# Placing the operands of the attention products 64 bytes apart modulo 128 in an fp32r kernel with split operands

## The chip, the cores and the metric

One core of a Trainium2 chip. The metric is the device time of one execution in microseconds (us), the median of several runs. TensorE (PE) does the matmuls, PEld is its weight load, VectorE is DVE, ScalarE is ACT, GpSimd is POOL. All runs quoted here were in the fast state, with a granted clock of 0.997 to 0.999. Ratios are the mean time of one kernel's fast runs over that of the other's of the same rounds, so not quite the ratio of the medians that stand beside them. The rounds of the experiments ran on three chips, so kernels of different rounds are compared through their ratios.

## The reference

```python
q = einsum('bwhc,cd->bwhd', x, Wq) + bq          # x: (4, 64, 64, 256), q and k: 128 channels
k = einsum('bwhc,cd->bwhd', x, Wk) + bk
v = einsum('bwhc,cd->bwhd', x, Wv) + bv
pq, pk, pv = (t.reshape(B, -1, 4096) for t in (q, k, v))
attention = softmax(einsum('bcn,bcm->bnm', pq, pk), axis=-1)
out = einsum('bcm,bnm->bcn', pv, attention).reshape(B, W, H, C)
return gamma * out + x
```

Four images, 4096 queries and 4096 keys each.

## The kernel before

Each operand is split in three forms, called h, l and d, of the program's type fp32r (the trace lists it as f32), and each product is made of three. For every image 16 groups of 256 queries are worked off, each in 8 **units** of 512 keys. One unit is 36 matmuls on TensorE: 12 of q·k (three forms, four key blocks), then 8 each of vh·h, vl·l and vd·d, in that order. In the matmul call the first argument after the output is the weights and the second is what is streamed, so k and h, l, d are weights and q and vh, vl, vd are streamed.

```python
VC = C + 4                                   # C = 256
...
pool("pad", 1).tile([P, 16], F32, name="pad")
ppool, work, kpool = pool("ppool", 2), pool("work", 2), pool("kpool", 3)
...
vh = qkv.tile([P, NM, VC], F32R, tag="vh", name="vh")
vl = qkv.tile([P, NM, VC], F32R, tag="vl", name="vl")
vd = qkv.tile([P, NM, C], F32R, tag="vd", name="vd")
...
def energy(b, u, k):                         # q.k, half a unit
    ...
    for i in range(2):
        for to, f, first, last in ((sa, 0, True, False), (sa, 1, False, True), (sb, 2, True, True)):
            nc.tensor.matmul(
                to[:, i], kt[:, 2 * k + i, f, :], q[:, :, f, :], start=first, stop=last
            )
...
def attend(b, u):                            # v.p, one unit
    ...
    for left, right in ((h, vh), (l, vl), (d, vd)):
        for j in range(NJ):                  # two blocks of 128 queries
            out_ = bb[:, j, :] if left is d else acc[j]      # acc is 258 wide, bb 256
            for i in range(4):
                m = 2 * t + i // 2 + NI * (i % 2)
                nc.tensor.matmul(
                    out_,
                    left[:, i, j * P : (j + 1) * P],
                    right[:, m, : out_.shape[1]],
                    ...
                )
```

Rows of vh and vl end in two columns of ones, which give the softmax sums. That is why their products have 258 columns and those of vd and q·k 256.

## Time and profile before

| | before |
|---|---|
| median | 2495.41 us (2495.35 to 2495.9) |
| PE busy, PEld busy | 99%, 98% |
| DVE, ACT busy | 85%, 73% |
| matmul records | 19,982, of them 18,432 in q·k and v·p |

The lines that carry this are in the prediction below. Two readings come before it. A busy time of PE is overlapped latency, so the pace has to be read from where matmuls start. And the timeline merges equal neighbours: a row says when the first of eight started, so the next row's start minus this one's, over eight, is the pace. These are the starts of vh in four successive units of the kernel before (timeline of TensorE, start us, us, engine, line, operation, tile and shape, count):

```profile
218.72 1.11 PE L368 MATMUL a<-vh,h 128*128 128x258 f32 x8
...
222.98 1.13 PE L368 MATMUL a<-vh,h 128*128 128x258 f32 x8
...
227.23 1.11 PE L368 MATMUL a<-vh,h 128*128 128x258 f32 x8
...
231.46 0.76 PE L368 MATMUL a<-vh,h 128*128 128x258 f32 x5
```

The units last 4.26, 4.25 and 4.23 us: they are not all alike. This small fact turned out to be the key.

### The profile page before, as it was taken

The page shows a single profiled execution, that of the slowest core. Times are in us where ns is not written, and L with a number is a line of the kernel's source. Part 1 is how long each engine was busy: PE and PEld are TensorE (multiplying, and loading weights), DVE is VectorE, ACT ScalarE, POOL GpSimd, SP SyncE. Part 2 cuts the span into 40 slices and gives each one's busy share as a digit, 9 for nine tenths or more (in the row PEclk, how much of TensorE's full clock was granted, in tenths as well). Part 3 has the DMA queues.
Part 4 walks back from the last instruction along what each step waited for, and adds up shares of the span by engine and source line. Part 5 has one row for each costly group of instructions (what it writes and reads, how often), then busy time and mean ns, then how long its engine had stood idle before and what let it go on. Part 6 is the DMA issues. An engine that isn't in the chain of part 4 may idle for free.

```text
span 2492.0 us, 50085 instructions
## 1 busy us (share of the span) xinstructions
PE 2478.3 (99%) x19982; PEld 2436.0 (98%) x19982; DVE 2108.0 (85%) x2440; ACT 1808.3 (73%) x3138; POOL 425.0 (17%) x780
## 2 busy tenths in 40 slices
PE   9999999999999999999999999999999999999998
PEld 8999999999899999999989999999998999999998
DVE  5888888888698888888869888888886988888887
ACT  5777777776677777777667777777766777777775
POOL 4211111111411111111041111111114111111110
PEclk9999999999999999999999999999999999999999
DMA  7766666664766666666477666666648666666663
GB/s 238 219 193 211 200 205 198 195 208 150 239 216 195 205 201 205 203 192 207 137 245 222 200 192 208 203 207 196 191 145 253 216 201 198 200 204 207 199 192 110
DMA packets 137408, 498.92 MB, mean 200 GB/s; under 512 B 15536, under 2 KB 57264, under 8 KB 137168
## 3 DMA queue, kind: packets, MB, share of 16 engines
q0 software_dynamic: 92320, 453.17, 57.8%
q1 hardware_dynamic: 44304, 42.22, 5.7%
q8 instruction: 160, 2.62, 0.4%
q14 instruction: 80, 0.66, 0.1%
q10 hardware_dynamic: 544, 0.26, 0.0%
HBM read 445.25 MB, written 50.33 MB: 199 GB/s over the span
## 4 chain that ended last, share of the span: by engine, by line
PE 97%; ACT 2%; DVE 1%; issue 0%; DMA 0%; SPq 0%; ACTq 0%; DVEq 0%
PE a L368 38%; PE sa L318 19%; PE bb L368 19%; PE sb L318 10%; PE qk L136 4%; PE v L157 4%; PE ot L414 1%; PE xt L123 1%; ACT h L337 1%; DVE x L332 1%; ACT x L322 0%; ACT y L322 0%; DMA x<-in_x_dram 0%; DVE vd L285 0%; ACT vh L282 0%
## 5 line engine op out<-in xcount | busy, mean ns | idle before, releaser
L322 ACT ACTIVATE x<-sa 128x512 f32<-128x512 f32 x1024 | 608.2, 594 | 399.7 <-PE sa L318 386.4
L318 PE MATMUL sa<-q,k 128*128 128x256 f32 x4096 | 755.0, 282 | 0.7 <-ACT x L322 0.7
L332 DVE TENSOR_TENSOR x<-x,y 128x1024 f32<-128x1024 f32 x512 | 625.3, 1221 | 152.9 <-ACT y L322 152.9
L318 PEld LDWEIGHTS sa<-q,k 128*128 128x128 f32 x4096 | 627.8, 189 | 2.1 <-ACT x L322 1.5
L343 DVE TENSOR_TENSOR l<-x,h 128x1024 fp32r<-128x1024 f32 x512 | 623.5, 1218 | 0.0
L346 DVE SCALAR_TENSOR_TENSOR d<-h,x 128x1024 fp32r<-128x1024 f32 x512 | 623.4, 1218 | 0.0
L322 ACT ACTIVATE y<-sb 128x512 f32<-128x512 f32 x1024 | 612.8, 598 | 0.0
L318 PE MATMUL sb<-q,k 128*128 128x256 f32 x2048 | 580.7, 284 | 0.0
L368 PE MATMUL a<-vh,h 128*128 128x258 f32 x4096 | 576.6, 283 | 0.0
L368 PE MATMUL a<-vl,l 128*128 128x258 f32 x4096 | 574.2, 283 | 0.0
L337 ACT ACTIVATE h<-x 128x1024 fp32r<-128x1024 f32 x512 | 543.6, 1062 | 41.1 <-DVE x L332 37.9
L368 PE MATMUL bb<-vd,d 128*128 128x256 f32 x4096 | 559.9, 279 | 0.0
L302 POOL DMA_DIRECT2D k<-kf x512 | 280.0, 547 | 1485.3 <-PE sb L318 1466.7
L368 PEld LDWEIGHTS a<-vl,l 128*128 128x128 f32 x4096 | 526.9, 190 | 0.0
L368 PEld LDWEIGHTS a<-vh,h 128*128 128x128 f32 x4096 | 524.0, 189 | 0.0
L368 PEld LDWEIGHTS bb<-vd,d 128*128 128x128 f32 x4096 | 515.1, 189 | 0.0
L318 PEld LDWEIGHTS sb<-q,k 128*128 128x128 f32 x2048 | 385.4, 188 | 9.6 <-ACT y L322 3.3
L136 PE MATMUL qk<-wqk_sb,xts 128*128 128x256 f32 x512 | 121.3, 380 | 0.0
L398 DVE SCALAR_TENSOR_TENSOR o<-a,o 128x256 f32<-128x256 f32 x126 | 47.5, 419 | 87.2 <-ACT o L378 87.2
L157 PE MATMUL v<-xts,wv_sb 128*128 128x256 f32 x512 | 120.3, 379 | 0.0
L157 PEld LDWEIGHTS v<-xts,wv_sb 128*128 128x128 f32 x512 | 97.3, 190 | 13.2
L406 ACT ACTIVATE o<-o,r 128x256 f32<-128x256 f32 x126 | 57.4, 503 | 72.4 <-DVE r L389 72.4
(54 smaller groups left out, 927.7 us busy)
## 6 DMA issues: line engine op xcount, KB each, us to landing
k<-kf POOLq DMA_DIRECT2D x512, 768.0 KB, 4.7
x<-in_x_dram SPq DMA_DIRECT2D x128, 256.0 KB, 3.7
kf<-f POOLq DMA_DIRECT2D x64, 384.0 KB, 3.9
out_dram<-x POOLq DMA_DIRECT2D x63, 256.0 KB, 2.5
qd<-qks POOLq DMA_DIRECT2D x128, 64.0 KB, 3.0
qr<-qd SPq DMA_DIRECT2D x64, 128.0 KB, 3.0
wv_sb<-in_L_conv_Wv_dram POOLq DMA_DIRECT2D x1, 256.0 KB, 6.1
out_dram<-x SPq DMA_DIRECT2D x1, 256.0 KB, 3.7
```

Of the source, the lines that this page charges most:

```text
L136: nc.tensor.matmul(qk[:, s, :], self.xt[i][:, k, s, :], wqk_sb[:, k, :], start=(k == 0), stop=(k == KC - 1),)
L157: nc.tensor.matmul(vp[:, eh, :], wv_sb[:, k, eh * P : (eh + 1) * P], self.xt[i][:, k].rearrange("p s a -> p (s a)"), start=(k == 0), stop= ...
L302: nc.gpsimd.dma_start(t.rearrange("p (i s) f d -> p i s (f d)", s=2), kf[b, u % NU])
L318: nc.tensor.matmul(to[:, i], kt[:, 2 * k + i, f, :], q[:, :, f, :], start=first, stop=last)
L322: nc.scalar.activation(to[:, 2 * k : 2 * k + 2, :], sp.rearrange("p i j d -> p i (j d)"), AF.Exp, scale=scale,)
L332: nc.vector.tensor_tensor(x, x, y, ALU.mult)
L337: nc.scalar.activation(h, units[b, u], AF.Identity, scale=UPPER)
L343: nc.vector.tensor_tensor(l, x, h.bitcast(F32), ALU.subtract)
L346: nc.vector.scalar_tensor_tensor(d, h.bitcast(F32), 1.0 + E, x, ALU.mult, ALU.subtract)
L368: nc.tensor.matmul(out_, left[:, i, j * P : (j + 1) * P], right[:, m, : out_.shape[1]], start=(t == i == 0 and (left is h or left is d and ...
L398: nc.vector.scalar_tensor_tensor(o[:, j, :], a[:, :C], 1.0 + E, o[:, j, :], ALU.mult, ALU.add)
L406: nc.scalar.activation(o[:, j, :], o[:, j, :], AF.Identity, scale=r[:, j : j + 1])
```

## The change

The intent: make the distance between the two operands of every product 64 bytes modulo 128. Rows of 1152 bytes for vh and vl take 7 KB per partition more, so k's forms move into buffers of l and d, which are free while k is made, and the raw q has one buffer instead of two.

```diff
-    VC = C + 4
+    VC = C + 32
...
-        ppool, work, kpool = pool("ppool", 2), pool("work", 2), pool("kpool", 3)
+        ppool = pool("ppool", 2)
+        pool("pad2", 1).tile([P, 16], F32, name="pad2")
+        work, kpool = pool("work", 2), pool("kpool", 3)
...
-            f = kpool.tile([P, 2, 3, P], F32R, tag="f", name=f"f_{b}_{i}", bufs=2)
+            f = ppool.tile([P, 4, NB], F32R, tag="ld"[i % 2], name=f"f_{b}_{i}")
+            f = f.rearrange("p i n -> p (i n)")[:, : 6 * P]
+            f = f.rearrange("p (s j d) -> p s j d", s=2, j=3)
...
-            t = work.tile([P, NJ, P], F32, tag="qr", name=f"qr_{b}_{g}")
+            t = work.tile([P, NJ, P], F32, tag="qr", name=f"qr_{b}_{g}", bufs=1)
```

Start addresses modulo 128 in the built programs: before, vd 32, vh and vl 32 plus 16 per row, h, l and d 96, q 96, k 32; after, vd, vh and vl 32, h, l and d 96, q 32, k 96.

## The prediction

> **What bounds the kernel now.** I read, in this order, the page's busy shares, the chain that ended last, the costliest groups, a stretch table, and then the timeline of TensorE. The first two name the engine:
>
> ```profile
> PE 2478.3 (99%) x19982; PEld 2436.0 (98%) x19982; DVE 2108.0 (85%) x2440; ACT 1808.3 (73%) x3138; POOL 425.0 (17%) x780
> ...
> PE 97%; ACT 2%; DVE 1%; issue 0%; DMA 0%; SPq 0%; ACTq 0%; DVEq 0%
> ```
>
> TensorE is never without work, its weight loads are under way 98% of the time, and 97% of the last chain is matmuls. So the time is the number of matmuls times the pace at which they follow one another. The groups that carry it:
>
> ```profile
> L318 PE MATMUL sa<-q,k 128*128 128x256 f32 x4096 | 755.0, 282 | 0.7 <-ACT x L322 0.7
> L318 PE MATMUL sb<-q,k 128*128 128x256 f32 x2048 | 580.7, 284 | 0.0
> L368 PE MATMUL a<-vh,h 128*128 128x258 f32 x4096 | 576.6, 283 | 0.0
> L368 PE MATMUL a<-vl,l 128*128 128x258 f32 x4096 | 574.2, 283 | 0.0
> L368 PE MATMUL bb<-vd,d 128*128 128x256 f32 x4096 | 559.9, 279 | 0.0
> ```
>
> These are 6,144 matmuls of q·k and three times 4,096 of v·p, 18,432 of all 19,982. The 280 ns are latency with overlap, not pace. The pace is in the stretch table for 700 to 1200 us (columns: busy us and count of PE, PEld, DVE, ACT, POOL, then clock, DMA share, GB/s) and in the timeline of TensorE (start us, us, engine, line, tile, count):
>
> ```profile
> 700.00:1200.00 500.00, 499.83 (x4202) 497.44 (x4202) 437.91 (x479) 373.93 (x635) 71.01 (x129) 1.00 0.65 201
> ```
>
> ```profile
> 1010.97 1.11 PE L368 MATMUL a<-vh,h 128*128 128x258 f32 x8
> 1011.91 1.11 PE L368 MATMUL a<-vl,l 128*128 128x258 f32 x8
> 1012.86 1.11 PE L368 MATMUL bb<-vd,d 128*128 128x256 f32 x8
> 1013.81 0.40 PE L318 MATMUL sa<-q,k 128*128 128x256 f32 x2
> ```
>
> 500 us / 4202 is 119.0 ns per matmul, with the clock at 1.00. In this timeline eight vh products take 0.94 us from their start to the next group's, eight vl 0.95, eight vd 0.95. I then took start-to-start times of all single records, leaving out intervals over 135 ns (waits), and set them beside the addresses the built program gives the operands: vd 116.5 ns, q·k 117.0, vh 119.6, vl 119.9. In vd and q·k the streamed rows and the weights already lie 64 bytes apart modulo 128 (vd at 32, d at 96; q at 96, k at 32). In vh and vl they do not: a row is 260 floats, 1040 bytes, so each row's start moves by 16 bytes modulo 128 and every distance occurs. That difference of some 3 ns is what the change is after.
>
> Two finer observations decide how large I think it is. First, the paces of vd and q·k are not one number: they are either 113, 113, 114 in long runs, or 117, 118, 118 in long runs, hardly anything between. 39% of vd's intervals and 18% of q·k's are at 114 or less; of vh's 3%, of vl's 5%. Within a run of the fast kind, the weight load for the next product starts 3 or 4 ns after a product starts and the next product follows 110 ns after that; in the slow kind it is 114 or 115. It looks like two rhythms, each of which keeps itself. Second, the step from vd's last product to k's next weights (vd at 32, k at 32, distance 0) is 118.9 on average and **never** under 117, and in the records I read a fast run of vd ends exactly there.
>
> **What the Trainium skill says.** "TensorE: Matmul & The Clock Gate", LDWEIGHTS, gives a weight load as its columns over 1.2 GHz: 128 columns are 106.7 ns, an estimate by that page; its Weight-path perf modes section says fast weight load is off for FP32. The trace agrees that loads set the rhythm (a product starts 110 to 120 ns after its own load did), and 119.0 ns is about 12 over that floor. "Perfetto Trace Analysis", Identifying the Most-Contended Engine, says to judge TensorE by LDWEIGHTS busy share and not by matmul busy time; here 98% says the same. "SBUF — State Buffer", Who interferes with whom, gives PE two independent read ports and says PE never waits on anyone. By that page the distance between operands can cost nothing and the change should be worth zero. The trace disagrees weakly: 116.5 and 117.0 against 119.6 and 119.9.
>
> **The change, part by part.** The order of instructions is the same on all engines: 19,469 matmul instructions in the same sequence before and after, none added or removed. What changes is places.
>
> Rows of vh and vl are now 288 floats, 1152 bytes, nine times 128, so every row starts at 32 and h and l stay at 96: always 64 apart. The second pad moves q to 32 and k to 96: still 64 apart, but now vd (32) to k (96) is 64 apart too, and q (32) to h (96), which was 0. All of this is on the path, because TensorE is.
>
> Cost of room: k's forms f go into the buffers of l and d, and the raw q has one buffer. f had two buffers and has four now, so it waits less (the waits show ACT f on its own store for 8.3 us in total, off the chain). The new duties are that l and d of an image's first two units wait for the stores of the last f, 3.9 us to landing; issued some units earlier, I take them at 0 to 2 us per image. The raw q is loaded two units before it is used and again six units later, so one buffer suffices. Together **0 to +5 us**.
>
> Gain if vh and vl merely become what vd is (vd's 116.5, and 0.8 for two more columns at 2.4 GHz: 117.3): 4096 x (2.3 + 2.6) ns = 20 us, and 500 steps from vd to k x 2.7 ns = 1.4 us. Sum **21 us**, giving 2474.
>
> Gain if half of all products fall into the fast rhythm (256 columns 115.6; 258 columns 116.8, as 115 is the pace at which vl repeats itself when it does): q·k 6144 x 1.4 = 8.6, vd 4096 x 0.9 = 3.7, vh 4096 x 2.8 = 11.5, vl 4096 x 3.1 = 12.7. Sum **36 us**, giving 2459.
>
> Gain if nothing throws the rhythm any more (113.4 and 115): q·k 22, vd 13, vh 19, vl 20. Sum **74 us**, giving 2422.
>
> **The rivals.** (a) Distance does not matter and the 3 ns have another cause. For it: those vh products that by chance lie 64 apart have a median of 119, no better than those at 48 or 96. Against it: their neighbours lie 80 apart, and a rhythm needs a long run to settle. It would give 2485 to 2497. (b) Another engine takes over. VectorE is busy 437.91 of 500 us, so it has 12% left; the full gain would shorten the attention stretch by 3.5%, VectorE would be at some 91%. ScalarE has 25%. Neither becomes the bound, but the groups have waits already (about 0.35 us of each 34.7 us period around the first unit of a query group, where scores wait for ScalarE), and a faster TensorE reaches them earlier; that may eat a quarter of the gain. (c) All products settle into the slow rhythm: vh and vl gain 2 ns, vd loses 1.2; about 2485. (d) The new sharing of buffers makes a wait in front of each image; four images at 2 us would not exceed 8 us.
>
> **Range and chances.** I weigh little or nothing (2487) at 0.2, the vd-like case (2474) at 0.3, half (2459) at 0.25, all (2422) at 0.25: mean 2460. I choose 2457, since someone went to this trouble for room. Two per cent is 50 us, 2445.5, which needs about two thirds of the full gain: 0.36. Slower by 2% has no mechanism of that size: 0.01. Range 2415 to 2488.
>
> **What would show it.** In the profile after: the same counts; PE still at 99% and the chain nearly all PE; eight vh and eight vl products from start to start at 0.92 to 0.94 us; vd to k no longer always over 117; more runs at 113 in q·k, whose share I put at half. No group of ACT or DVE should take over the chain, and idle of VectorE before l should stay at nearly 0. I am wrong if vh and vl stay at 119 to 120 (distance is not the cause), if vd and q·k slow down (address phase against ScalarE's and VectorE's own accesses matters), or if waits of scores for ScalarE grow by as much as the products gain.

## The result, and the profile after

The changed kernel takes **2504.14 us** (2502.99 to 2504.99, 4 runs) against 2495.38 (2495.07 to 2495.9): ratio 1.0035, 95% interval 1.0017 to 1.0052. It is slower, by a third of a per cent, where 1.5% faster was forecast. The result is correct.

The page after: busy shares, then the five groups of matmuls that the prediction shows (columns as there; line numbers are five higher).

```profile
PE 2490.1 (99%) x19982; PEld 2447.4 (98%) x19982; DVE 2107.9 (84%) x2440; ACT 1806.8 (72%) x3138; POOL 424.7 (17%) x780
...
L323 PE MATMUL sa<-q,k 128*128 128x256 f32 x4096 | 758.7, 283 | 0.8 <-ACT x L327 0.3
...
L323 PE MATMUL sb<-q,k 128*128 128x256 f32 x2048 | 583.0, 285 | 0.0
L373 PE MATMUL a<-vl,l 128*128 128x258 f32 x4096 | 578.8, 284 | 0.0
L373 PE MATMUL a<-vh,h 128*128 128x258 f32 x4096 | 575.9, 283 | 0.0
...
L373 PE MATMUL bb<-vd,d 128*128 128x256 f32 x4096 | 560.7, 279 | 0.0
```

Counts are the same, TensorE is as full as before, DVE has not grown (2107.9 against 2108.0 us). The part of the page with the last chain is empty for this run, so it can't be compared. The stretch table for 700 to 1200 us:

```profile
700.00:1200.00 500.00, 499.60 (x4177) 496.74 (x4176) 435.64 (x476) 371.56 (x633) 70.44 (x128) 1.00 0.65 202
```

4177 matmuls where there were 4202: 119.7 ns each instead of 119.0. So the loss is pace, spread over the whole span. Now the timeline of TensorE, three units:

```profile
221.06 1.11 PE L373 MATMUL a<-vh,h 128*128 128x258 f32 x8
222.01 1.13 PE L373 MATMUL a<-vl,l 128*128 128x258 f32 x8
222.98 1.09 PE L373 MATMUL bb<-vd,d 128*128 128x256 f32 x8
223.91 0.40 PE L323 MATMUL sa<-q,k 128*128 128x256 f32 x2
...
225.33 1.12 PE L373 MATMUL a<-vh,h 128*128 128x258 f32 x8
...
229.60 1.12 PE L373 MATMUL a<-vh,h 128*128 128x258 f32 x8
```

The units now last 4.27 and 4.27 us. In the single records this is much sharper. I took the units that have no interval over 135 ns (a wait), from the first q·k product to the next unit's first:

```
            units   mean ns   values that occur (ns: times)
before       368    4252.7    4280: 58, 4214: 50, 4253: 41, 4258: 40, 4272: 36, 4233: 36, ...
after        366    4271.8    4273: 231, 4274: 112, 4272: 9, 4232: 8, ...
```

Before, each unit has two row distances for vh and vl, and the pair changes from unit to unit through four; units take half a dozen different times. After, every unit but a few takes 4273 ns, to the nanosecond. 4271.8 less 4252.7 is 19.1 ns, times 512 units 9.8 us: the loss (8.8 us between the medians). The intervals of one unit, median over the repeats, in the order q·k (12), vh, vl, vd (8 each):

```
after, each of units 3 and 5 of a group, to a nanosecond
  117 119 118 118 118 117 118 117 118 118 117 123 | 119 123 121 116 121 116 121 119
  117 127 118 121 123 119 122 121 | 121 114 123 118 113 113 113 113
before, unit 5
  114 118 118 118 118 118 117 118 117 118 118 117 | 118 118 120 128 116 118 121 116
  121 126 122 119 118 123 115 115 | 113 113 113 113 113 113 113 118
before, unit 3
  114 118 118 117 118 117 118 118 117 118 118 118 | 124 116 117 113 119 119 120 122
  121 122 118 123 115 119 120 122 | 122 120 118 118 118 117 118 122
```

And the pace of each kind (mean start to start, counted with the product that starts the interval, so that a hand-over falls to the earlier kind; intervals over 135 ns left out; "fast" is the share at 114 ns or less):

| | before | after |
|---|---|---|
| q·k | 117.0, fast 18% | 117.9, fast 5% |
| vh | 119.6 | 119.5 |
| vl | 119.9 | 121.0 |
| vd | 116.5, fast 39% | 116.6, fast 51% |

With waits included the sums move by q·k +5.1 us, vh -0.7, vl +4.5, vd +0.4, together +9.3 us. Which kind bears the loss depends on this way of counting: counted with the product that ends the interval, q·k goes from 115.8 to 116.0 ns, vh from 119.2 to 119.6, vl from 120.0 to 120.9 and vd from 116.5 to 117.3. The sum is the same.

### The profile page after: what moved, and what is told of

Same layout as the page of the kernel before. It is cut to its first block, busy times and chain, and to the rows that moved or that the text cites. A ratio compares the mean times of both kernels' runs of the same rounds, so it can differ in the third digit from the quotient of the medians.

```text
span 2503.2 us, 50079 instructions
## 1 busy us (share of the span) xinstructions
PE 2490.1 (99%) x19982; PEld 2447.4 (98%) x19982; DVE 2107.9 (84%) x2440; ACT 1806.8 (72%) x3138; POOL 424.7 (17%) x780
## 4 chain that ended last, share of the span: by engine, by line
## 5 line engine op out<-in xcount | busy, mean ns | idle before, releaser
L157 PE MATMUL v<-xts,wv_sb 128*128 128x256 f32 x512 | 120.3, 379 | 0.0
```

The lines of the kernel that those rows point to most:

```text
L157: nc.tensor.matmul(vp[:, eh, :], wv_sb[:, k, eh * P : (eh + 1) * P], self.xt[i][:, k].rearrange("p s a -> p (s a)"), start=(k == 0), stop= ...
```

## The experiments

Each is an edit of the changed kernel unless said otherwise. In all of them TensorE stays busy 99% of the span. Medians of the changed kernel are compared through the ratios to before (changed: 1.0035).

### Which part loses: rows, q, or room

`only_rows` leaves the second pad out, so that q stays at 96 and k at 32.

```diff
-        pool("pad2", 1).tile([P, 16], F32, name="pad2")
```

> The change without the second pad: vh and vl rows 288 floats apart, so 64 apart from h and l; q stays at 96 and k at 32 as before. Theory A (the distance modulo 128 is what sets a product's pace, and moving q spoiled it): vh and vl take 117 ns from start to start, the time is 2470 to 2485. Theory B (the width of 258 columns, not the distance, is what makes vh and vl slow): vh and vl stay at 119 to 121, the time is 2492 to 2502. Theory C (the loss comes from moving q): no slower than before, 2488 to 2497, q.k at 117.0 and its step to h at 117.

Measured: 2505.29 us, ratio 1.0042 (1.0025 to 1.0059). vh 119.8, vl 121.1. All 366 units without waits take 4273 or 4274 ns. The time missed all three ranges, by 3 us for theory B, which had the pace. So the rows alone make the whole loss and the uniform unit. The theory that moving q spoiled a gain is out.

`only_q` keeps the old rows:

```diff
-    VC = C + 32
+    VC = C + 4
```

> The change with the old row of 260 floats: q at 32 and k at 96, k's forms in the buffers of l and d. Theory A: vd to k loses its kick, a small gain, 2485 to 2494. Theory B: within 5 us of before. Theory C (the loss comes from moving q): 2500 to 2506, with q.k near 117.6 and the step from q.k to h near 121.

Measured: 2497.27 us, ratio 1.0009 (1.0002 to 1.0016), hardly a loss. Units take a mix of times again, mean 4252.5 as before. The step from q·k to h is slower (120.1 against 117.1) as that theory said, but vd gains (115.8), and the sum is next to nothing.

`room_only` has neither the pad nor the rows, only k's forms in the buffers of l and d and one raw q:

```diff
-    VC = C + 32
+    VC = C + 4
-        pool("pad2", 1).tile([P, 16], F32, name="pad2")
```

> Only the saving of room: k's forms in l's and d's buffers and one buffer of raw q; rows of 260 floats and q at 96 as before. All theories but one: within 3 us of before, same unit times. Rival G (the sharing of buffers costs a wait per image, and is part of the loss): 4 to 10 us slower, with waits on the store of f before l and d.

Measured: 2496.43 us, ratio 1.0005 (0.9997 to 1.0014), units mean 4252.7. Room costs nothing that shows.

### Is it the distance?

`zero_apart` puts both operands of every product of q·k and v·p at 32: the first pad goes, and a pad between work and kpool takes the place of the second.

```diff
-        pool("pad", 1).tile([P, 16], F32, name="pad")
         ppool = pool("ppool", 2)
-        pool("pad2", 1).tile([P, 16], F32, name="pad2")
-        work, kpool = pool("work", 2), pool("kpool", 3)
+        work = pool("work", 2)
+        pool("pad3", 1).tile([P, 16], F32, name="pad3")
+        kpool = pool("kpool", 3)
```

> The changed kernel with both operands of every product of q.k and v.p at the same place modulo 128 (all at 32). Theory A (64 apart is the good distance, 0 the bad one): every product is slower, 120 ns or more, 2525 to 2600. Theory B: the same as the changed kernel within 8 us, 2496 to 2512, with vd and q.k at 116 to 118.

Measured: 2521.24 us, ratio 1.0105 (1.0088 to 1.0122). It missed both forecasts, lying between them. vd 119.7 (+3.1 on the changed kernel), vh 121.5 (+2.0), q·k 118.6 (+0.7), but vl 119.9 (-1.1). Every unit 4313 or 4314 ns. So 0 is worse than 64 on the whole, and not for every kind.

`v_0`, `v_32` and `v_112` change the distance of vh and vl only, by beginning v's rows 16, 24 or 12 floats later in their 288. For `v_112`:

```diff
-            nc.scalar.copy(t[:, :, C : C + 2], ...)
+            nc.scalar.copy(t[:, :, 12 + C : 12 + C + 2], ...)
-            h = vh[:, m, :C]
+            h = vh[:, m, 12 : 12 + C]
-            for t, f in ((vl, 1.0 / E), (vd, 1.0 / E + 1.0)):
+            for t, f, o in ((vl, 1.0 / E, 12), (vd, 1.0 / E + 1.0, 0)):
                 nc.vector.scalar_tensor_tensor(
-                    t[:, m, :C], ...
+                    t[:, m, o : o + C], ...
-                            right[:, m, : out_.shape[1]],
+                            right[:, m, :C] if left is d else right[:, m, 12 : 12 + C + 2],
```

> The changed kernel with v's rows begun 12 floats later, so that vh and vl lie 112 modulo 128 from h and l; vd and q.k stay at 64. Before the change 53% of vl's intervals at distance 112 were 115 ns. Theory E (with 258 columns another distance than 64 is the good one, and 112 is): vl at 115 to 117, 2480 to 2494. Rival F (258 columns find no short rhythm at any distance): vh and vl at 119 to 121, 2496 to 2508.

> The same with 24 floats, distance 32 for vh and vl. Theory A (64 is best, others worse): vh and vl slower than 120.3 and 121.0, 2508 to 2525. Theory F (no distance matters much at 258 columns): 2496 to 2508.

> The changed kernel with v's rows begun 16 floats later: vh and vl at distance 0 from h and l, the rest at 64. If distance counts for 258 columns: vh and vl 122 or more, 2512 to 2525. If not, like distances 32 and 112: pooled pace of vh and vl 119.5 to 120.5, 2495 to 2506.

| distance of vh and vl | time | ratio | vh, vl, their mean | unit ns |
|---|---|---|---|---|
| 0 (v_0) | 2507.53 | 1.0051 (1.0034 to 1.0068) | 121.6, 119.7, 120.65 | 4280 |
| 32 (v_32) | 2501.32 | 1.0024 (1.0015 to 1.0034) | 118.6, 120.7, 119.7 | 4267 |
| 64 (changed kernel) | 2504.14 | 1.0035 (1.0017 to 1.0052) | 119.5, 121.0, 120.25 | 4273 |
| 112 (v_112) | 2499.18 | 1.0014 (1.0007 to 1.0021) | 119.4, 120.3, 119.85 | 4260 |
| all in turn (before) | | 1 | 119.6, 119.9, 119.75 | mixed, mean 4253 |

`v_32` and `v_112` fell in the ranges of theory F; `v_0` lies between its two forecasts. For products of 258 columns 64 is not the good distance; the means differ by 1 ns over the whole range (vh alone by 3.0, vl by 1.3). Each uniform distance gives nearly every unit one time, and those lie above before's mean. My hope for 112 (vl at 115 in 53% of such intervals before) came to nothing: next to other neighbours the same distance gives another pace.

`vd_zero` moves vd alone, to 96 where d is, with all else in place:

```diff
-        ppool = pool("ppool", 2)
+        vdpool, ppool = pool("vdpool", 1), pool("ppool", 2)
-        vd = qkv.tile([P, NM, C], F32R, tag="vd", name="vd")
+        vd = vdpool.tile([P, NM, C], F32R, tag="vd", name="vd")
```

> The changed kernel with vd moved to 96, distance 0 from d, vh, vl and q.k as they are. If distance counts for 256 columns: vd at 119 to 120, 12 to 20 us slower, 2514 to 2526. If the slow vd of zero_apart came from how its stretch was entered: vd at 116 to 118, 2500 to 2510.

Measured: vd 119.6 as forecast, yet the kernel is **faster** than the changed one: 2500.12 us, ratio 1.0018 (1.0010 to 1.0027). The interval overlaps that of the changed kernel, but the units without waits take 4254.2 ns on average instead of 4271.8. The first forecast has the pace of vd and not the time; the time lies at the edge of the second's range, whose pace did not come. The timeline of TensorE shows where the rest comes from:

```profile
221.14 1.12 PE L373 MATMUL bb<-vd,d 128*128 128x256 f32 x8
222.09 0.40 PE L323 MATMUL sa<-q,k 128*128 128x256 f32 x2
...
223.48 0.76 PE L373 MATMUL a<-vh,h 128*128 128x258 f32 x5
```

Here vd takes 0.95 us and the twelve q·k products 1.39; in the fence of the changed kernel above, vd takes 0.93 and q·k 225.33 less 223.91, 1.42. In the records q·k is at 115.0 ns with 66% fast, against 117.9 and 5%, though its own operands lie exactly as in the changed kernel. Sums with waits: vd +12.5 us, q·k -17.3. Distance counts for vd itself (3 ns). That the slower vd hands over to q·k in a state from which q·k falls into its fast rhythm is inferred: the step from vd to k lies at distance 0 again here, and no run tells the two apart.

### Is it the width, or the cut in q's stream?

`w256` lets vh and vl products be 256 wide. The softmax sums are missing, so the output is wrong on purpose, and the range check is opened so that the fallback isn't taken.

```diff
-    Z_LOW, Z_HIGH = 2.0**-60, 2.0**80
+    Z_LOW, Z_HIGH = -(2.0**120), 2.0**120
-            out_ = bb[:, j, :] if left is d else acc[j]
+            out_ = bb[:, j, :] if left is d else acc[j][:, :C]
-                            right[:, m, : out_.shape[1]],
+                            right[:, m, :C],
-            nc.vector.tensor_copy(zall[...], a[:, C : C + 1])
+            nc.vector.tensor_copy(zall[...], a[:, C - 1 : C])
```

> The changed kernel with vh and vl products of 256 columns instead of 258, wrong on purpose (no sums, so wrong scale of the output), all distances 64. Theory B (width): vh and vl fall to vd's pace of 113 to 117, the time falls by 25 to 60 us to 2440 to 2480. Theory A says nothing but 0.8 ns for two columns less: 7 us less, 2497. If neither width nor distance matters, 2495 to 2498 with vh and vl at 119 to 120.

Measured: 2485.23 us, ratio 0.9962 (0.9948 to 0.9976). It missed all its forecasts: five us above theory B's range, ten below the others. vh 117.9, vl 117.5: 1.6 and 3.5 ns less than at 258, where two columns are worth 0.5 to 0.7 ns (an estimate from the 14 columns of `w272` below). They come to what vd has in this run, 117.7. The stretch table shows the rise in pace, 4218 matmuls where the changed kernel had 4177:

```profile
700.00:1200.00 500.00, 499.61 (x4218) 496.11 (x4217) 439.12 (x481) 375.61 (x637) 71.40 (x130) 1.00 0.64 203
```

The same trace holds the plainest evidence for what comes later. Addresses modulo 128 and widths are the same in all its units, and still the units take two times in turn (starts of vh, timeline of TensorE):

```profile
220.16 1.11 PE L373 MATMUL a<-vh,h 128*128 128x256 f32 x8
...
224.40 1.10 PE L373 MATMUL a<-vh,h 128*128 128x256 f32 x8
...
228.60 1.11 PE L373 MATMUL a<-vh,h 128*128 128x256 f32 x8
```

That is 4.24 and then 4.20 us. In the single records 182 units without waits take 4239 or 4240 ns and 182 take 4206 or 4207, and in all 296 pairs of successive ones the time changes from one to the other. Waits shift the turn, so units of even and of odd number, and with them both buffers of l and d, show both times. What differs is what the unit before left behind; whether in TensorE alone, no run shows.

`w256_rows260` is the same edit on `only_q`, that is with the old rows.

> The old rows of 260 floats with q moved, and vh and vl products of 256 columns (wrong on purpose), to set beside the same width with rows of 288 (2485.2). If 64 apart is good for products of 256 columns only, this is 5 to 20 us slower than that, 2490 to 2505, with vh and vl at 118.5 or more against 117.9 and 117.5. If distance matters at neither width, 2480 to 2487.

Measured: 2484.51 us, ratio 0.9957 (0.9941 to 0.9974), vh 118.2, vl 118.0. So at 256 columns, too, rows at a uniform 64 win no time. vh and vl gain 0.3 and 0.5 ns, and vd loses more (117.7 against 115.8). Against `only_q`, the same rows at 258 columns, the width is worth 1.9 ns for vh and 1.5 for vl.

`w272` goes the other way, to 16 columns of ones:

```diff
-            nc.scalar.copy(t[:, :, C : C + 2], ones[:, : 2 * NM].rearrange("p (m t) -> p m t", t=2))
+            nc.scalar.copy(t[:, :, C : 272], ones[:, :1].unsqueeze(2).to_broadcast([P, NM, 272 - C]))
-                    ps_o.tile([P, C + 2], F32, ...)
+                    ps_o.tile([P, 272], F32, ...)
```

> The changed kernel with vh and vl products of 272 columns (16 columns of ones instead of 2), correct. 14 columns more are 5.8 ns[...] if the stream sets the pace: 125.8 for vh and 126.9 for vl, 2550. If the weight load sets it and 258 is slow only since it breaks the rhythm of 64-byte pieces (272 floats are 17 whole ones): 116 to 119, 2475 to 2500.

Measured: 2534.91 us, ratio 1.0160 (1.0143 to 1.0177). The time lies between the forecasts. vh 124.7, vl 124.2, which is 5.2 and 3.2 ns more for 14 columns, nearer the first. So the stream counts in the pace, not the weight load alone. Here, too, units of the same addresses and widths take one of two times, about 4327 or 4353 ns, and keep it: in 282 of 298 pairs of successive units without waits it is the same.

`q_whole` stores q form by form, so that each score product streams one piece.

```diff
-            t = work.tile([P, NJ, 3, P], F32R, tag="q", name=f"q_{b}_{g}")
+            t = work.tile([P, 3, NJ, P], F32R, tag="q", name=f"q_{b}_{g}")
+            t = t.rearrange("p f j d -> p j f d")
```

> The changed kernel with q stored form by form, so that a score product streams 256 floats in one piece instead of two pieces of 128 that lie 1536 bytes apart. Theory D (the cut in q's stream throws q.k out of the rhythm of 113 ns into the one of 117.7): q.k falls to 113 to 115 and keeps vd's rhythm, 2478 to 2490. Rival: the cut does nothing, q.k stays at 117 to 118, 2498 to 2507.

Measured: 2505.58 us, ratio 1.0043 (1.0026 to 1.0059), q·k 117.8, and the median intervals of a unit are those of the changed kernel within a nanosecond. The theory of the cut fell.

### Is it the order?

`d_first` puts vd ahead in each unit; no address, width or count differs.

```diff
-            for left, right in ((h, vh), (l, vl), (d, vd)):
+            for left, right in ((d, vd), (h, vh), (l, vl)):
```

> The changed kernel with the vd products ahead of vh and vl in each unit; no address, width or count differs. Theory H (the rhythm is decided by the state in which a stretch of products is entered): unit time moves by 15 to 80 ns from 4273, either way, the same in all units: 2465 to 2497 or 2510 to 2530. Rival (each kind of product has its pace by address and width alone): within 4 us of the changed kernel.

Measured: 2479.98 us, ratio 0.9936 (0.9920 to 0.9953). q·k goes from 117.9 to 115.4 (67% fast), vd from 116.6 to 117.8 (1% fast): now q·k stands where the rhythm settles and vd where it is disturbed. All but 3 of 368 units without waits take 4253 or 4254 ns, 18 to 19 ns less than the changed kernel's mean. This is some 9.5 of the 24 us. The larger half is another thing: intervals over 135 ns exceed the pace by 15.4 us instead of 28.5 (12.5 instead of 24.1 of them in q·k), as bb is complete 16 products earlier and is copied out earlier. ScalarE's waits for bb fit this, first in the changed kernel, then in `d_first` (us in total, times, longest us):

```profile
ACT o L383 <- PE bb L373: 56.0, 63, 5.2
...
ACT o L383 <- PE bb L373: 9.6, 3, 3.2
```

That this is why TensorE waits less is argued from the order and these waits, not tested apart.

`d_first_old` is the same edit in the kernel **before**.

> The same reordering in the kernel before. Theory H: paces of q.k and vd move by over 0.5 ns, the time by 5 us or more either way. Rival: within 4 us of before, 2491 to 2499.

Measured: **2471.78 us** (2471.61 to 2472.32), ratio 0.9906 (0.9889 to 0.9922), correct: the fastest kernel of this study that is correct. q·k 114.9 with 66% fast, units mean 4237.3 instead of 4252.7, and waits shorter by some 12 us. Its stretch table:

```profile
700.00:1200.00 500.00, 499.81 (x4253) 499.42 (x4252) 441.46 (x481) 375.97 (x643) 71.44 (x131) 1.00 0.65 204
```

4253 matmuls in the 500 us where before has 4202.

`d_first_q` is that with q moved to 32 (the edit of `d_first` on `only_q`).

> Rows of 260 floats, q moved to 32, vd first. If 64 apart everywhere but in vh and vl is best: q.k keeps 113 through vd, 2450 to 2470, faster than d_first_old's 2471.8. If entry states decide case by case: 2465 to 2485.

Measured: 2479.79 us, ratio 0.9939 (0.9923 to 0.9956), q·k 116.2 with 40% fast. More pairs at 64 did not help here either.

`l_first_old` swaps the two kinds of 258 columns in the kernel before, and the start and stop marks with them.

```diff
-            for left, right in ((h, vh), (l, vl), (d, vd)):
+            for left, right in ((l, vl), (h, vh), (d, vd)):
-                            start=(t == i == 0 and (left is h or left is d and j == 0)),
-                            stop=(t == NU - 1 and i == 3 and left is not h),
+                            start=(t == i == 0 and (left is l or left is d and j == 0)),
+                            stop=(t == NU - 1 and i == 3 and left is not l),
```

> The kernel before with the vl products ahead of vh; waits should stay as they are (excess near 24 us on q.k). Theory H: paces of single stretches move, the time by 3 to 15 us either way. Rival (pace by address and width alone): within 2 us of before.

Measured: 2495.84 us, ratio 1.0000 (0.9992 to 1.0009), so my forecast from theory H missed and the rival's number held. The reason is plain afterwards: vh and vl both begin at 32 and h and l at 96, so the swap leaves the sequence of addresses modulo 128 as it was. The paces swap places with the names (first kind 119.5, second 119.9) and the unit times are before's, 4280, 4214, 4258, 4253, 4233, 4273. Other buffers, elsewhere in memory, but the same sequence modulo 128 and of widths: the same pattern. It fits theory H only in the form that what counts is the sequence, and it shows that the names do not matter, nor the address bits from 512 bytes up (the buffers of vh and vl lie 33,280 bytes apart in the built program). Whether 128 is the right modulus, and not 256, no run tests.

## Why the prediction was wrong, point by point

**The bound** was right: TensorE at 99%, the same counts, no other engine took over.

**Room** was right: forecast 0 to 5 us, `room_only` shows 1.0005.

**The step that failed** is "if vh and vl merely become what vd is": 20 us from 2.3 and 2.6 ns. They came to 64 apart and stayed: vh 119.5 (0.1 ns gained), vl 121.0 (1.1 lost), in sum 3.8 us lost. I had laid the 3 ns between vd and vh or vl to the distance, but they differ in three more things: width, place in the unit and the PSUM tile that they add to. In `w256` the width is worth 1.6 and 3.5 ns, with the old rows 1.9 and 1.5. `d_first` shows the place: moved to the front, with the same address and width, vd is at 117.8 and nearly never fast. The sweep from `v_0` to `v_112` shows what distance is worth at 258 columns: under 1 ns in the mean of vh and vl, with 64 not the best. The PSUM tile was not tested apart; in `w256` vh, vl and vd all run at 117.5 to 117.9 with their different tiles. Distance is real for vd (119.6 against 116.6 in `vd_zero`), and there it was already 64. I had noticed that vh products which happened to be 64 apart were no faster, and explained it away by their neighbours. The 0.8 ns for two more columns came from no run; `w272` puts it at 0.5 to 0.7.

**That weight loads set the rhythm** I read from the time between a load and its product, 110 to 120 ns. But loads run one product ahead, so this time is near the pace whatever sets the pace. `w272` shows that the streamed columns count too.

**The two rhythms** of 113 and 117.7 exist. What throws a stretch into one or the other was wrong. The step from vd to k did lose its kick, 118.9 to 113.7 ns, 2.3 us, more than the 1.4 forecast. But q·k behind it became slow nearly always (fast 18% to 5%), where I forecast half, and the step from q·k to h, which I counted as improved, went from 117.1 to 121.2. `vd_zero` is the sharpest counter-case: with distance 0 brought back at that step, and in vd, q·k is fast 66% of the time.

**What stands in its place.** In the changed kernel a unit takes 4273 or 4274 ns in nearly all cases, though ScalarE and VectorE start between 8 and 11 instructions in it, at different times, and `l_first_old` keeps the pattern of before with other buffers. `w256` has two unit times for one sequence, strictly in turn. So within a stretch without waits the pace follows from the sequence of operand addresses (modulo 128 as far as tested) and widths, and from the state in which it is entered; it is not a property of each product. Before, row distances changed from unit to unit and units ran at 4214 to 4280 ns, 4252.7 on average. Uniform rows replaced this mix by one pattern, 4273, which happens to lie above that mean. The 19 ns, times 512, are the loss.

**Rival (a)**, that distance does not matter, with 2485 to 2497, came nearest, and I gave it too little weight. It had the direction of the truth for 258 columns and not the loss.

The Trainium skill, "SBUF — State Buffer", Who interferes with whom, which says PE never waits on anyone, would have given nearer to the truth than my reading. Still `vd_zero` does not fit it: a move of one operand by 64 bytes cost vd 3 ns.

**Open:** what in the hardware makes the two rhythms, and why 258 columns cost more than two columns' worth. No run here looks inside a matmul. Why uniform rows settle above the mean of the mixed ones is not explained either. Which pattern a sequence settles in I could not foresee in any case here; the hand-overs were only found by running them.

## What to carry to other kernels

A difference between two groups of a trace is not the effect of the one property you have in mind; list what else differs (here width and place in the sequence) and change one of them alone before rebuilding the layout around it. Where TensorE is the bound, the order of independent products is a free knob worth trying before addresses: putting one kind of product first gave 0.94% with one line, the placement lost 0.35% with many. Of the 24 us of that gain some 8 (15.4 ns in 512 units) are pace and some 12 shorter waits.

## What the Trainium skill lacked or had wrong

- "SBUF — State Buffer", Who interferes with whom: the read ports of PE for the streamed operand and the weights are called independent, and PE is said never to wait on anyone. Moving one streamed operand (vd) from 64 to 0 bytes from its weights modulo 128 took its products from 116.6 to 119.6 ns; the page says nothing on such distances.
- "TensorE: Matmul & The Clock Gate", Back-to-back issue gap: for streams of weight loads and matmuls, where it says that both set the spacing, it gives about 81 ns at 128 columns and 131 at 512, and none between. fp32r products with a new weight load each ran at 113.3 or 117.7 ns in steady stretches of 256 columns here, about 120 at 258 columns and 124.5 at 272.
- No page says that the pace of a matmul depends on what ran just before it, apart from the clock gate, and the granted clock was 1.00 here: the same q·k products, at the same addresses, ran at 117.9 or 115.0 ns by what vd's address was, and in `w256` units of the same addresses and widths took 4240 and 4207 ns in turn.
